# Second GIN pass of a graph network kernel: the second weight product for four chunks at a time

## The chip, the cores and the metric

The kernel runs on one core of one Trainium2 chip. The metric is the device time of one execution in microseconds. Nine plain executions of the kernel before took 5144.92 to 5174.38 us, with a median of 5162.2 us. Besides these there is one profiled execution, and every row quoted from the profile comes from it.

The engines are called as the profile calls them: PE is TensorE's matrix product (PEld its weight load), DVE is VectorE, ACT is ScalarE, POOL is GpSimd, SP is SyncE, which here only issues transfers. A name with q behind it (SPq) is the engine's sequencer.

## The reference

A graph has 6250 nodes with 256 features and 100,000 edges, sorted by destination. Two layers follow one another, each as `x = x + layer(relu(layernorm(x)))`. The first is an attention layer with batch norms. The second, which the change touches, is three graph convolutions (GIN):

```
def _gin_conv(h, src, dst, w, b, eps, n_nodes):
    agg = jax.ops.segment_sum(h[src], dst, num_segments=n_nodes)
    return ((1.0 + eps) * h + agg) @ w + b
h = relu(_gin_conv(x, src, dst, w1, b1, eps1, n))    # 256 -> 512
h = relu(_gin_conv(h, src, dst, w2, b2, eps2, n))    # 512 -> 512
return   _gin_conv(h, src, dst, w3, b3, eps3, n)     # 512 -> 256
```

For each node the features of all its neighbours are added up, its own features are added, and the sum goes through a weight matrix.

## The kernel before

The edges are cut into 53 chunks (`NCK`), each of 15 tiles (`CK`) of 128 edges, so that one chunk covers the edges of at most 128 destination nodes. For one tile, POOL issues an indirect DMA that gathers the 128 source rows from a table in DRAM into a row buffer `g` (`gather`, line 538). DVE makes, once a chunk, the matrix `hot` (line 555) that has a one where an edge belongs to a node. A product of `hot` with the gathered rows, accumulated over the 15 tiles in `sum`, gives the neighbours' sum for the chunk's nodes (`neighbours`, the products at line 1121; in f32 each shows as two product instructions and two weight loads).

The second layer is done in three passes over the chunks. The pass of this study (pools `s3`) is the second: its table `g1_d` has rows of 512 f32 numbers, 2 KB, so a tile's gather brings 256 KB. For each chunk, in the order of the program:

- SP loads the chunk's own rows (`own_rows`, line 1134, five buffers) and the rows of the residual (`x1`, line 1260, six buffers).
- `neighbours` runs the 15 gathers and products, with 24 row buffers `g`.
- DVE adds the own rows to the neighbours' sum (line 1263) into `own`.
- A step `flip` transposes `own` on TensorE (line 1145, four tiles of 128 columns), and ACT copies the result into the chunk's quarter or half of `tt` (line 1146).

The pass also applies the second weights, and at once the third ones, which stand before the third sum (the sum of products is the product of the sum). That is done by `layer23` for two chunks together. It makes steps: four `two(f)`, each with one tile of 128 outputs of the second product for all the nodes of both chunks (`h_ps`, line 1224, four accumulated products of 256 columns, then a relu by ACT into `g2`, line 1227); and one `three(q)` a chunk, with the third product (`y_ps`, line 1234, one buffer). After that product ACT copies `y` (line 1238), `apart` splits it into three bf16 parts (lines 1102 to 1105, ACT and DVE in turn), SP stores the parts as rows of `y3_d` (line 1244), and DVE adds the bias `g_b3` to `x1` (line 1245), then `y` times (1 + eps) (line 1246), and SP stores the result in `base_d` (line 1247). `keep_rows` (line 1209) loads finished rows of `y3_d` back into `tab`, for the last pass.

The steps are not run where they are made. They are put on the list `work`, and `neighbours` takes one from it after the products of the tiles named in `between`, ten of a chunk's 15:

```
between = (2, 4, 5, 6, 7, 8, 10, 11, 12, 13)
...
            if j in between and work:
                work.pop(0)()
```

So a chunk's `flip` runs after the third tile of the next chunk. With pairs, the even chunk (the first of a pair) carries seven steps: the flip of the chunk before, four `two` and two `three`, at tiles 2, 4, 5, 6, 7, 8 and 10. The odd chunk carries one flip. What is left at the end runs after the last chunk.

The order of instructions on an engine follows the program, except that the planner which builds the program puts an instruction earlier when it takes its inputs to be there. In the trace of before, the bias addition of line 1245 is one of these: it needs only `x1` and the bias, and stands ahead of the row addition (line 1263) of a chunk. `tc.keep_in_program_order` puts an instruction behind everything that the program has already given its engine.

Gathers are issued in order by POOL. Each needs a free row buffer, which is one whose product has been done. The queue of SP holds the loads and the stores of the pass in one order.

Of the kernel before, what the change touches and what calls it, by code (L numbers as in the profile page):

```python
# [33 lines left out]
FT = mybir.dt.float32  # L34
# [3 lines left out]
OP = mybir.AluOpType  # L38
# [5 lines left out]
P = 128  # L44
NN = 6250
NE = 100000
D = 256
# [6 lines left out]
NCK = 53  # L54
# [50 lines left out]
def gnn_kernel(ctx: ExitStack, tc: tile.TileContext, a: dict, out: bass.AP):  # L105
# [391 lines left out]
    with branch.Else():  # L497
        chunked(tc, a, out, t)
# [3 lines left out]
def chunked(ctx, tc, a, out, t):  # L502

    nc = tc.nc
# [3 lines left out]
    vs_d, x1_d, g0_d, g1_d, y3_d, base_d = t.vs_d, t.x1_d, t.g0_d, t.g1_d, t.y3_d, t.base_d  # L508
    sizes = [P] * (NCK - 1) + [LASTW]

    def first_nodes():

        got = {}

        def of(c, engine):
            if c in (0, NCK - 1):
                return 0 if c == 0 else NN - LASTW
            if c % 8 == 0 or c == 1:
                c0, c1 = c // 8 * 8, min(c // 8 * 8 + 8, NCK)
                if (engine, c) not in got:  # L520
                    _, regs = nc.values_load_multi_w_load_instructions(
                        t.nodes[0:1, c0:c1],
                        engines=[engine],
                        min_val=0,
                        max_val=NN - P,
                        skip_runtime_bounds_check_because="chunks whose rows go past the end take the general path",
                    )
                    got[engine, c] = True
                    got[engine] = regs
            return got[engine][c % 8]  # L530

        return of

    def ds(node, c):
        return bass.ds(node, sizes[c])

    def gather(to, table, c, j):
        nc.gpsimd.indirect_dma_start(  # L538
            out=to,
            out_offset=None,  # L540
            in_=table,
            in_offset=bass.IndirectOffsetOnAxis(ap=src_c[:, c, j : j + 1], axis=0),
        )
# [8 lines left out]
    def one_hot(pool, rule, c, dtype=FT, **more):  # L552

        hot = pool.tile([P, CK, P], dtype, name="hot", **more)
        nc.vector.tensor_tensor(  # L555
            hot,
            rule[:, None, :P].to_broadcast([P, CK, P]),
            loc_c[:, c, :][:, :, None].to_broadcast([P, CK, P]),
            op=OP.is_equal,
        )  # L560
        return hot
# [24 lines left out]
    with (  # L586
# [70 lines left out]
        def apart(s, q):  # L657
            nc.scalar.activation(s.hot_t[:, edges_of(q)], s.loc_r[:, edges_of(q)], AF.Square, bias=minus_p)
# [316 lines left out]
    with tc.tile_pool(name="s1b", bufs=2) as sp, tc.tile_pool(name="s1b_ps", bufs=4, space=PSUM) as pp:  # L975
        w_2 = weight(sp, "w_2", [a["L0_gnn_W2"]])
        for n, (c0, w) in enumerate(parts):
# [4 lines left out]
            for f in range(4):  # L982
                ps = pp.tile([P, 512], FT, name="ps")
# [9 lines left out]
            for f in range(2):  # L993
                ps = pp.tile([P, 512], FT, name="ps2")
# [55 lines left out]
    g_b3 = row(wp, "g_b3", a["L1_gnn_b3"], D)  # L1050
    rule = ruler(ctx.enter_context(tc.tile_pool(name="l1_rule", bufs=1, space=PSUM)))[0]
    hots = []
# [40 lines left out]
    def three(ps, weights, rows, start, stop):  # L1093

        rows = rows.rearrange("p k d -> p (k d)")
        parts = [(ps, rows[:, : 2 * D]), (ps[:, D:], rows[:, 2 * D :])]
        for k in (0, 1) if start else (1, 0):
            nc.tensor.matmul(parts[k][0], weights, parts[k][1], start=start and k == 0, stop=stop and k == 0)  # L1098
# [8 lines left out]
    def neighbours(pool, psum, table, c, n, bufs, hots, work, dense=None, dtype=FT):  # L1107


        if dense and c in dense.cs:  # L1110
            return dense.sums.pop(c)
        if c == 0:
            hots.append(one_hot(pool, rule, 0, dtype))
        hot = hots.pop()
        ps = psum.tile([P, n if dtype == FT else 2 * D], FT, name="sum")
        following = c + 2 if dense and c + 1 in dense.cs else c + 1
        for j in range(CK):
            g = pool.tile([P, n], dtype, name="g", bufs=bufs)
            gather(g, table, c, j)
            if dtype == FT:  # L1120
                nc.tensor.matmul(ps, hot[:, j, :], g, start=j == 0, stop=j == CK - 1)  # L1121
            else:
                three(ps, hot[:, j, :], g.rearrange("p (k d) -> p k d", k=3), j == 0, j == CK - 1)
            if j == 9 and following < NCK:
                hots.append(one_hot(pool, rule, following, dtype))
            if j in between and work:
                work.pop(0)()
            if dense:
                dense.step()
        return ps  # L1130

    def own_rows(pool, table, c, n, node):
        t = pool.tile([P, n], FT, name="own", bufs=5)
        nc.sync.dma_start(t[: sizes[c]], table[ds(node, c), :])
        return t
# [15 lines left out]
    with tc.tile_pool(name="s2", bufs=2) as sp, tc.tile_pool(name="s2_ps", bufs=2, space=PSUM) as pp:  # L1151
# [19 lines left out]
        work = [partial(part_rows, b0) for b0 in range(0, NFB, 5)]  # L1171
# [15 lines left out]
        for c in range(NCK):  # L1187
            R = slice(0, sizes[c])
            node = first(c, EN.SP)
            own = own_rows(sp, g0_d, c, D, node)  # L1190
            ps = neighbours(sp, pp, g0_d, c, D, 30, hots, work, dense)
# [3 lines left out]
            tt = sp.tile([P, 2, P], FT, name="tt")  # L1195
# [9 lines left out]
    def keep_rows(done):  # L1205

        while left and (left[0] + 1) * FB <= done:
            b = left.pop(0)
            nc.sync.dma_start(tab[:FB, b].rearrange("p k d -> p (k d)"), y3_d[b * FB : (b + 1) * FB, :])

    with tc.tile_pool(name="s3", bufs=2) as sp, tc.tile_pool(name="s3_ps", bufs=2, space=PSUM) as pp:
        first = first_nodes()
        work = []

        def layer23(cs, tt, nodes, x1s):

            n = sum(sizes[c] for c in cs)
            g2 = sp.tile([P, 4, 2 * P], FT, name="g2", bufs=1)
            tt_f = tt.rearrange("p f q n -> p f (q n)")

            def two(f):
                h_ps = pp.tile([P, 2 * P], FT, name="h_ps")
                for k in range(4):
                    nc.tensor.matmul(  # L1224
                        h_ps[:, :n], g_w2[:, k, f * P : (f + 1) * P], tt_f[:, k, :n], start=k == 0, stop=k == 3
                    )
                nc.scalar.activation(g2[:, f, :n], h_ps[:, :n], AF.Relu, bias=g_b2[:, f : f + 1])

            def three(q):
                c, node, x1 = cs[q], nodes[q], x1s[q]  # L1230
                R = slice(0, sizes[c])
                y_ps = pp.tile([P, D], FT, name="y_ps", bufs=1)
                for k in range(4):
                    nc.tensor.matmul(  # L1234
                        y_ps[R], g2[:, k, q * P : q * P + sizes[c]], g_w3[:, k, :], start=k == 0, stop=k == 3
                    )
                y = sp.tile([P, D], FT, name="y")
                nc.scalar.copy(y[R], y_ps[R])  # L1238
                y3 = sp.tile([P, 3, D], BF, name="y3")
                rest = sp.tile([P, D], FT, name="rest")  # L1240
                apart(y_ps[R], [y3[R, k, :] for k in range(3)], rest[R])
                if c:
                    keep_rows(DONE[c])
                nc.sync.dma_start(y3_d[ds(node, c), :], y3[R].rearrange("p k d -> p (k d)"))
                nc.vector.tensor_tensor(x1[R], x1[R], g_b3[R], op=OP.add)
                nc.vector.scalar_tensor_tensor(x1[R], y[R], eps1[R, 2:3], x1[R], op0=OP.mult, op1=OP.add)  # L1246
                nc.sync.dma_start(base_d[ds(node, c), :], x1[R])

            return [partial(two, f) for f in range(4)] + [partial(three, q) for q in range(len(cs))]

        for c0 in range(0, NCK, 2):
            cs = list(range(c0, min(c0 + 2, NCK)))
            tt = sp.tile([P, 4, 2, P], FT, name="tt")
            nodes, x1s = [], []
            for q, c in enumerate(cs):
                R = slice(0, sizes[c])
                nodes.append(first(c, EN.SP))
                own = own_rows(sp, g1_d, c, 2 * D, nodes[q])
                x1 = sp.tile([P, D], FT, name="x1", bufs=6)
                nc.sync.dma_start(x1[R], x1_d[ds(nodes[q], c), :])  # L1260
                x1s.append(x1)
                ps = neighbours(sp, pp, g1_d, c, 2 * D, 24, hots, work)
                nc.vector.scalar_tensor_tensor(own[R], own[R], eps1[R, 1:2], ps[R], op0=OP.mult, op1=OP.add)  # L1263
                work.append(flip_of(sp, pp, c, own, tt[:, :, q]))
            work += layer23(cs, tt, nodes, x1s)
        for f in work:
            f()

    with tc.tile_pool(name="s4", bufs=2) as sp, tc.tile_pool(name="s4_ps", bufs=2, space=PSUM) as pp:
# [3 lines left out]
        for c in range(NCK):  # L1273
            R = slice(0, sizes[c])
            node = first(c, EN.SP)
            o = own_rows(sp, base_d, c, D, node)
            ps = neighbours(sp, pp, y3_d, c, 3 * D, 30, hots, [], dense, BF)
# [779 lines left out]
```

## Time and profile before

| what | us |
|---|---|
| median of nine plain executions | 5162.2 |
| profiled execution, its own time | 5185.4 |
| its span, first to last instruction | 5183.6 |
| second GIN pass, first gather | 3078.9 |
| last gather of that pass issued | 4344.0 |
| first gather of the third pass | 4385.2 |
| PE busy in the span | 3496.0 |
| POOL busy in the span | 2819.9 |
| DVE busy in the span | 1644.2 |

In the profile, an instruction group or a timeline row names line, engine, operation, what is written and read, shape and count; times are the start in us and the length in us. In square brackets stands the time for which the engine stood idle before it, and what ended that: an instruction, a transfer (DMA), "issue" where the profile shows no wait, or "remote" where a semaphore changed at that time and the profile can't name who changed it. The ends of PE's products are modelled.

### The profile page before, as it was taken

The page shows a single profiled execution, that of the slowest core. Times are in us where ns is not written, and L with a number is a line of the kernel's source. Part 1 is how long each engine was busy: PE and PEld are TensorE (multiplying, and loading weights), DVE is VectorE, ACT ScalarE, POOL GpSimd, SP SyncE. Part 2 cuts the span into 40 slices and gives each one's busy share as a digit, 9 for nine tenths or more (in the row PEclk, how much of TensorE's full clock was granted, in tenths as well). Part 3 has the DMA queues.
Part 4 walks back from the last instruction along what each step waited for, and adds up shares of the span by engine and source line. Part 5 has one row for each costly group of instructions (what it writes and reads, how often), then busy time and mean ns, then how long its engine had stood idle before and what let it go on. Part 6 is the DMA issues. An engine that isn't in the chain of part 4 may idle for free.

```text
span 5183.6 us, 43522 instructions
## 1 busy us (share of the span) xinstructions
PE 3496.0 (67%) x14077; PEld 2104.0 (41%) x14077; DVE 1644.2 (32%) x3806; ACT 784.5 (15%) x1689; POOL 2819.9 (54%) x2947
## 2 busy tenths in 40 slices
PE   6725554555554008937888877888888887677777
PEld 3414433443433004625555544444444444233333
DVE  6536666666654004422111111111211211111111
ACT  2223333332332002211000000101101101000000
POOL 1355555554556760066666655565556554666665
PEclk8856777767776559968999998889989988788888
DMA  5466444443433002265555546676666665666665
GB/s 159 126 211 197 125 115 124 120 123 111 126 110 86 1 0 54 80 189 156 150 147 149 149 133 188 201 208 196 200 206 207 195 199 152 192 191 188 197 187 151
DMA packets 367412, 777.64 MB, mean 150 GB/s; under 512 B 83852, under 2 KB 197210, under 8 KB 366172
## 3 DMA queue, kind: packets, MB, share of 16 engines
q0 software_dynamic: 171120, 495.03, 33.6%
q1 hardware_dynamic: 172395, 261.51, 16.5%
q10 hardware_dynamic: 23658, 18.21, 1.2%
q8 instruction: 113, 1.85, 0.2%
q14 instruction: 126, 1.03, 0.1%
HBM read 703.07 MB, written 93.83 MB: 154 GB/s over the span
## 4 chain that ended last, share of the span: by engine, by line
PE 42%; another core or an unknown queue 20%; issue 16%; DVE 12%; DMA 6%; POOL 2%; ACT 2%; SPq 1%; ACTq 0%; DVEq 0%; POOLq 0%
PE dense L1098 10%; PE sum L1121 9%; PE sum L1098 4%; PE h_ps L1224 4%; PE acc L848 3%; DVE g L838 2%; PE g_ps L1179 2%; POOL g L538 2%; PE ps L985 2%; PE ps L996 2%; DVE junk L235 2%; PE y_ps L1234 1%; PE qk_ps L472 1%; DMA x<-x_d 1%
## 5 line engine op out<-in xcount | busy, mean ns | idle before, releaser
L538 POOL DMA_INDIRECT g<-g_d,src_t x1350 | 1287.9, 954 | 1137.0 <-PE sum L1121 319.8
L1121 PE MATMUL sum<-g,hot 128*128 128x512 f32 (+1 forms) x2700 | 1106.7, 531 | 59.8 <-DMA rows<-g_d 30.6
L538 POOL DMA_INDIRECT g<-vs_d,src_t x795 | 766.1, 964 | 682.4 <-issue 249.6
L848 PE MATMUL acc<-g,hot 128*128 128x264 f32 x1590 | 621.1, 546 | 514.1 <-DVE g L838 272.2
L1098 PE MATMUL dense<-tab,times 125*128 125x256 bf16 (+1 forms) x3300 | 792.0, 350 | 120.1 <-issue 116.9
L1121 PEld LDWEIGHTS sum<-g,hot 128*128 128x128 f32 x2700 | 532.7, 200 | 408.4 <-issue 352.2
L538 POOL DMA_INDIRECT g<-y_d,src_t x540 | 510.3, 945 | 307.9 <-PE dense L1098 113.8
L848 PEld LDWEIGHTS acc<-g,hot 128*128 128x128 f32 x1590 | 413.2, 278 | 610.0 <-DVE g L838 280.7
L1098 PEld LDWEIGHTS <-times 125*128 125x128 bf16 x3300 | 335.2, 103 | 457.0 <-issue 274.0
L1098 PE MATMUL sum<-g,hot 128*128 128x512 bf16 (+1 forms) x1080 | 303.6, 366 | 91.0 <-issue 68.9
L555 DVE TENSOR_TENSOR hot<-ruler,loc_t 128x1920 f32<-128x1920 f32 (+1 forms) x126 | 270.7, 2150 | 35.7 <-remote 13.1
L1224 PE MATMUL h_ps<-tt,g_w 128*128 128x256 f32 (+1 forms) x864 | 225.0, 408 | 61.8 <-issue 30.9
L1146 ACT COPY tt<-tp 128x256 f32<-128x256 f32 (+2 forms) x106 | 50.6, 478 | 1303.0 <-remote 673.3
L838 DVE TENSOR_TENSOR g<-g,at_ps 128x1024 f32<-128x1024 f32 x212 | 243.2, 1152 | 8.8 <-ACT at_ps L829 7.1
L1279 DVE TENSOR_TENSOR own<-own,sum 128x256 f32<-128x256 f32 (+1 forms) x72 | 30.0, 417 | 675.6 <-PE dense L1098 444.2
L253 POOL DMA_INDIRECT times<-val_t,at_t x210 | 205.1, 977 | 64.0 <-issue 64.0
L1224 PEld LDWEIGHTS h_ps<-tt,g_w 128*128 128x128 f32 x864 | 175.3, 209 | 156.7 <-issue 96.0
L1179 PE MATMUL g_ps<-g_w,tt 128*128 128x512 f32 (+1 forms) x212 | 133.7, 764 | 106.5 <-ACT tt L1146 59.0
L1098 PEld LDWEIGHTS <-hot 128*128 128x128 bf16 x1080 | 112.9, 106 | 210.7 <-issue 157.5
L1246 DVE SCALAR_TENSOR_TENSOR x<-y,eps,x 128x256 f32<-128x256 f32 (+1 forms) x53 | 25.7, 485 | 543.7 <-ACT y L1238 543.7
L1145 PE MATMUL tp<-ident,own 128*128 128x128 f32 (+1 forms) x318 | 65.2, 324 | 183.9 <-DVE own L1263 115.9
L677 PE MATMUL flip<-ident,s_e 128*120 128x128 f32 x53 | 18.6, 352 | 218.0 <-ACT s_e L672 187.2
(212 smaller groups left out, 3380.4 us busy)
## 6 DMA issues: line engine op xcount, KB each, us to landing
times<-times SPq DMA_DIRECT2D x165, 312.5 KB
loc_r<-loc_d SPq DMA_DIRECT2D x53, 480.0 KB
times<-zeros_d SPq DMA_DIRECT2D x14, 1562.5 KB
g<-g_d,src_t POOLq DMA_INDIRECT x1350
keys<-key_d SPq DMA_DIRECT2D x51, 384.0 KB
g_d<-g SPq DMA_DIRECT2D x52, 256.0 KB
own<-g_d SPq DMA_DIRECT2D x52, 256.0 KB
g<-vs_d,src_t POOLq DMA_INDIRECT x795
```

The costliest lines, as they stand in the source:

```text
L235: nc.vector.scalar_tensor_tensor(junk, keys[:, j * P : (j + 2) * P], key[:, q * 5 + j : q * 5 + j + 1], weigh, op0=OP.is_equal, op1=OP.mul ...
L253: return nc.gpsimd.indirect_dma_start(out=times_d[c], out_offset=bass.IndirectOffsetOnAxis(ap=at, axis=0), in_=val, in_offset=None)
L538: nc.gpsimd.indirect_dma_start(out=to, out_offset=None, in_=table, in_offset=bass.IndirectOffsetOnAxis(ap=src_c[:, c, j : j + 1], axis=0),)
L555: nc.vector.tensor_tensor(hot, rule[:, None, :P].to_broadcast([P, CK, P]), loc_c[:, c, :][:, :, None].to_broadcast([P, CK, P]), op=OP.is_e ...
L838: nc.vector.tensor_tensor(rows, rows, s.w_e[:, j0 // 8, j0 % 8 : j0 % 8 + n, :, None].to_broadcast([P, n, H, C]), op=OP.mult,)
L848: nc.tensor.matmul(s.acc, s.hot[:, j, :], s.g[:, j, :], start=j == 0, stop=j == CK - 1)
L985: nc.tensor.matmul(ps[:, :w], w_1[:, k, f * P : (f + 1) * P], h_t[:, k, c0 : c0 + w], start=k == 0, stop=k == 1,)
L996: nc.tensor.matmul(ps[:, :w], w_2[:, k, f * P : (f + 1) * P], hid[:, k, :w], start=k == 0, stop=k == 3)
L1098: nc.tensor.matmul(parts[k][0], weights, parts[k][1], start=start and k == 0, stop=stop and k == 0)
L1121: nc.tensor.matmul(ps, hot[:, j, :], g, start=j == 0, stop=j == CK - 1)
L1179: nc.tensor.matmul(g1_ps[R], tt[:, k, R], g_w1[:, k, :], start=k == 0, stop=k == 1)
L1224: nc.tensor.matmul(h_ps[:, :n], g_w2[:, k, f * P : (f + 1) * P], tt_f[:, k, :n], start=k == 0, stop=k == 3)
```

## The change

Three edits, all in the second GIN pass. `layer23` is given four chunks instead of two, so `h_ps`, `g2` and `tt` are twice as wide and the products at line 1224 have 512 columns; 53 chunks make 13 groups of four and one last chunk alone. To hold that, the row buffers go from 24 to 15, and the `x1` buffers from six to nine. And the bias addition is kept in its place in the program, behind the splitting of the product `y`.

```
         def layer23(cs, tt, nodes, x1s):
 
             n = sum(sizes[c] for c in cs)
-            g2 = sp.tile([P, 4, 2 * P], FT, name="g2", bufs=1)
+            g2 = sp.tile([P, 4, 4 * P], FT, name="g2", bufs=1)
             tt_f = tt.rearrange("p f q n -> p f (q n)")
 
             def two(f):
-                h_ps = pp.tile([P, 2 * P], FT, name="h_ps")
+                h_ps = pp.tile([P, 4 * P], FT, name="h_ps")
...
                 nc.sync.dma_start(y3_d[ds(node, c), :], y3[R].rearrange("p k d -> p (k d)"))
-                nc.vector.tensor_tensor(x1[R], x1[R], g_b3[R], op=OP.add)
+
+                tc.keep_in_program_order(nc.vector.tensor_tensor(x1[R], x1[R], g_b3[R], op=OP.add))
                 nc.vector.scalar_tensor_tensor(x1[R], y[R], eps1[R, 2:3], x1[R], op0=OP.mult, op1=OP.add)
...
-        for c0 in range(0, NCK, 2):
-            cs = list(range(c0, min(c0 + 2, NCK)))
-            tt = sp.tile([P, 4, 2, P], FT, name="tt")
+        for c0 in range(0, NCK, 4):
+            cs = list(range(c0, min(c0 + 4, NCK)))
+            tt = sp.tile([P, 4, 4, P], FT, name="tt")
...
-                x1 = sp.tile([P, D], FT, name="x1", bufs=6)
+                x1 = sp.tile([P, D], FT, name="x1", bufs=9)
...
-                ps = neighbours(sp, pp, g1_d, c, 2 * D, 24, hots, work)
+                ps = neighbours(sp, pp, g1_d, c, 2 * D, 15, hots, work)
```

With groups of four, the first chunk of a group carries nine steps: the flip of the chunk before, four `two` and four `three`, at tiles 2, 4, 5, 6, 7, 8, 10, 11 and 12. The other three chunks carry one flip each.

## The prediction

> **What bounds the kernel now.** The page first: 5183.6 us of span, 5185.4 us for the profiled execution. The nine plain times have a median of 5162.2 us, so the execution that I read is 0.45% above it, and the sum below is made against 5185.4 and then moved down by 23.
>
> ```profile
> span 5183.6 us, 43522 instructions
> PE 3496.0 (67%) x14077; PEld 2104.0 (41%) x14077; DVE 1644.2 (32%) x3806; ACT 784.5 (15%) x1689; POOL 2819.9 (54%) x2947
> PE   6725554555554008937888877888888887677777
> ```
>
> The change touches the second GIN pass alone, which runs from the first gather of `g1_d` at 3078.9 us to about 4385 us, a quarter of the span. Inside it I read the starts of the row addition at L1263, one a chunk. From chunk 4 (3227.65) to chunk 50 (4335.05) they are 1107.4 us apart, 48.15 us for two chunks. The two are unlike: 20.4 us on average from an even chunk's addition to the odd one's, where TensorE runs only gather products (L1121) and a transposition, and 27.7 us from odd to even, where the weight products of the pair before (L1224, L1234) lie between the gather products. Busy time by stretch, for one odd chunk, the even one after it, and the odd chunk 51, in which the last gathers end:
>
> ```profile
> 3707.95:3729.62 21.67, 15.85 (x40) 6.85 (x38) 3.67 (x5) 0.58 (x1) 15.10 (x16) 0.94 0.85 260
> 3729.62:3755.22 25.60, 23.20 (x77) 15.12 (x78) 5.30 (x9) 4.58 (x11) 13.22 (x14) 0.92 0.55 159
> 4335.05:4348.37 13.32, 13.32 (x35) 6.09 (x34) 2.82 (x3) 0.58 (x1) 7.57 (x8) 1.00 0.80 247
> ```
>
> The columns are length, then PE, PEld, DVE, ACT, POOL, clock, DMA share, GB/s. In the even chunk TensorE is nearly full. In the odd chunk it has 15.9 us of records in 21.7. Chunk 51 does an odd chunk's work in 13.3 us. The timeline shows why the others take 8 us more:
>
> ```profile
> 3710.76 13.04 PE L1121 MATMUL sum<-g,hot 128*128 128x512 f32 x30
> 3724.92 0.94 POOL L538 DMA_INDIRECT g<-g_d,src_t  x1 [0.89 <-PE sum L1121]
> 3727.03 0.94 POOL L538 DMA_INDIRECT g<-g_d,src_t  x1 [1.17 <-remote]
> 3729.62 0.75 DVE L1263 SCALAR_TENSOR_TENSOR own<-own,eps,sum 128x512 f32<-128x512 f32 x1 [3.49 <-remote]
> 3730.51 1.08 PE L1145 MATMUL tp<-ident,own 128*128 128x128 f32 x4 [6.71 <-issue]
> ...
> 4337.86 13.04 PE L1121 MATMUL sum<-g,hot 128*128 128x512 f32 x30
> 4348.37 0.75 DVE L1263 SCALAR_TENSOR_TENSOR own<-own,eps,sum 128x512 f32<-128x512 f32 x1 [10.50 <-PE sum L1121]
> ```
>
> Of the 30 products from 3710.76, 24 end the odd chunk (at about 3721.1) and six open the next, and then TensorE must transpose the odd chunk's `own`. L1263 needs the chunk's last product, but starts at 3729.6, 8.5 us after it; TensorE stands 6.7 us. What L1263 waits for, shown as remote, is the semaphore that counts TensorE's work, and POOL waits on it too. In chunk 51 the same 24 products end at 4348.2 and L1263 starts at once: POOL issued its last gather at 4344.0. So TensorE's completions become visible late while gathers are issued without pause (every 1.25 us, from about 3705.6), not otherwise. In even chunks, where POOL stands in front of full buffers, the delay is 0.6 us. Gathered rows are not what is missing: gather 390, issued at 3694.41, is used at 3721.06. I call the delay the late count; its cause is not in the trace.
>
> **The change, part by part.**
>
> *Wider product.* Eight h products of 256 columns take 1.73 us (3741.24 to the next gather product at 3742.97); 30 of 512 columns take 12.88, so eight take 3.43. Four chunks need 64 x 0.216 = 13.8 us of h products now and 32 x 0.429 = 13.7 us after. Nothing is gained: each weight load (0.19 us) already lies beside a product. The Trainium skill, page "TensorE: Matmul & The Clock Gate", section "Back-to-back issue gap", gives a sustained spacing of 81 ns at 128 columns and 131 ns at 512, less than in proportion. By that law 256 columns cost some 98 ns (an estimate), and the halved count would save a third of the 13.8 us, 60 us over 13 groups; the rows contradict it for this f32 product, and I go by the rows.
>
> *Where the dense work goes.* Now one chunk in two carries it; after, one in four, as nine steps (flip, four `two`, four `three`) in the ten slots. TensorE's work for four chunks, at full clock, is 51.5 (gather products) + 13.8 + 6.9 (y) + 1.7 (transpositions) = 73.9 us; now they take 2 x 48.15 = 96.3. Each odd chunk so loses 11.2 us: 7.1 in itself (20.4 against 13.3) and 4.0 in the chunk after (27.7 against 23.7; late copies of the transposed rows, slow clock after standing). After the change, for a group:
> - the dense chunk: 12.9 + 13.7 + 6.9 + 0.4 = 33.9; 4.0 of loss as now; and `y_ps` has one buffer, freed 1.43 us after the product (3700.87 to 3702.30), while after the change only one gather's products (0.86) lie between the second and third and the third and fourth `three`: 2 x 0.57 = 1.1. Sum 39.0.
> - the first gather-only chunk, as an odd chunk: 20.4.
> - the second and third, which no row shows: each follows a chunk that has itself stood. Lower end 15 x 1.25 = 18.75, POOL's unbroken pace with no late count to speak of. Upper end 28.5, the addition-to-addition time of the first two chunks of this pass (3111.11 to 3139.58), both gather-only. I take the odd chunk, the nearest row, 20.4, plus a slow start: after standing, four gather products took 3.06 us (3731.39) against 1.71, so 1.35 more: 21.8.
>
> Together 39.0 + 20.4 + 43.6 = 103.0 against 96.3: +6.7 us for each of 13 groups, +87 us. The ends: 96.9 gives +8 us, 116.4 gives +261.
>
> That slow start is the clock gate: the clock falls after the gap. The same page, Part 1, states half clock after about 3.4 us idle, and another 3.4 us of activity to leave it, 1.7 us lost each time instead of 1.35 (estimate); by it the two chunks cost 0.7 more a group, +9 us in all.
>
> *15 row buffers instead of 24.* A gather's rows are used under 5 us after its issue when TensorE waits for them (first issue 3078.92, first product 3083.78), and now rows lie landed for 20 us and more. 15 buffers are a whole chunk ahead. POOL's need is 60 x 1.25 = 75 us a group, less than 96. Taken at nothing; if the late count vanished, this would be the next bound. Lower end: POOL standing earlier shortens the late count (in the 18.75 above). Upper end: in the startup POOL ran 42 gathers before it stood, so fewer buffers bound nothing worse than 28.5.
>
> *Bias addition pinned.* Now L1245 runs ahead on DVE and waits for the `x1` load (11.39 us at 3725.7), in front of L1263. Over the pass DVE waits 331 us there, but L1263 then still waits for TensorE's count in 50 of 53 chunks, and the waits of TensorE put down to L1245 are 6.7 us, one. Gain: 7 us at least by that row, at most the three chunks times 11.4 = 34; I take 7. After the pin, L1245 (0.42) follows L1105 and precedes L1246, so the split of `y` (L1103, L1105) no longer stands behind L1246 and the base store goes out 1 us later; hidden by SP, which waits for the `tab` load anyway.
>
> *SP's queue.* The `y3` store, its `tab` load and the next `y3` store wait for each other: 3703.22, 3706.57, 3712.79, 3717.51, some 9.6 us a chunk. Four in a row hold the queue for 40 us; behind them are `own` and `x1` loads. `own` has five buffers, so a load comes four chunks ahead (some 80 us): hidden. `x1` with nine buffers reuses one that was stored a group earlier: hidden. At the end of the pass gathers have stopped, and a chunk's chain takes 5.8 us (4367.31 to 4373.10): four from the dense part of chunk 52 end near the last products; +2 us.
>
> *ACT.* L1227 on 512 columns costs as L1146's 0.58 us instead of 0.47, beside 3.4 us of product: nothing.
>
> Sum: +87 - 7 + 2 = +82; 5267 against the profiled execution, 5244 against the median. I say 5240.
>
> **The rivals.**
> - *POOL stands sooner and the late count shrinks (same or faster).* For it: with chunk 51, and the 0.6 us behind even chunks, the delay needs unbroken gathers, and 15 buffers end a run of gathers 9 earlier. Against: now, too, POOL starts an odd chunk at its buffer limit. Decides below: it ends faster once the two later gather-only chunks fall under 18.5 each; with the first one at 18.75 too, and 1.35 of clock, 39.0 + 3 x 18.75 = 95.3, -13 us, 5149; with no loss at all POOL's 75 us, -21 x 13 = -277, 4885. I expect some -60 in this case.
> - *Startup regime (much slower).* Gather-only chunks keep TensorE waiting and cold; 28.5 us twice a group: +261, 5420. For it: the two first chunks. Against: POOL had 24 free buffers then and no bound.
> - *The bias wait was the real stop.* If L1245 caused the stands, the pin would remove 7 us from each of 26 odd chunks, -180 us, and the group would win. Against: L1263 waited on TensorE 3.5 us longer than on DVE in the chunk shown, and chunk 0's addition came at 3111.1, its products having ended at 3101.4, with DVE idle since 3092.4.
> - *Nothing moves:* lower end of the third term, +8 us.
>
> **How the numbers follow.** Main case 0.55 (5190 to 5300), startup-like 0.13, near nothing 0.08, sooner-standing POOL 0.19, bias wait 0.05. A measurement tells some 0.2%, 10 us, from no change. Slower 0.69, same 0.08, faster 0.23. The range leaves out about one in ten on each side: below 5110 most of the strong gains, above 5350 the full startup regime.
>
> **What would show it.** L1263's starts in groups of one long (39) and three short gaps (20 to 22); TensorE standing 5 to 7 us before three of four transpositions, released as remote; 448 h products of twice the length and unchanged busy time; no L1245 wait for `x1`; gathers waiting for TensorE. Wrong if short gaps are below 18.5, if TensorE waits for gathers (buffers too few), or if SP's loads come late.

## The result, and the profile after

The changed kernel takes 5214.12 us (median of 17 executions, 5172.98 to 5233.29), the kernel before 5167.15 (median of 54): ratio 1.0084, 95% interval 1.0068 to 1.0101. So it is slower, by 47 us by the medians where 78 were forecast, and inside the range. The profiled execution took 5214.28 us, with these lines on its page:

```profile
span 5212.5 us, 42688 instructions
PE 3483.7 (67%) x13661; PEld 1985.1 (38%) x13661; DVE 1641.8 (31%) x3806; ACT 770.8 (15%) x1637; POOL 2816.5 (54%) x2947
PE   6634545555553129768888877788788787677777
```

TensorE has 12 us less to do than before (3496.0), and the span is 29 us longer. The pass as a whole, from its first gather to its last row addition, by stretch; first the kernel before, then the changed one (columns: stretch, length, then busy us and instructions of PE, PEld, DVE, ACT, POOL, then clock, DMA share, GB/s):

```profile
3078.90:4372.00 1293.10, 1069.70 (x3046) 596.20 (x3046) 234.28 (x314) 134.11 (x312) 752.65 (x795) 0.90 0.67 198
```

```profile
3053.20:4394.90 1341.70, 1064.36 (x2626) 483.30 (x2627) 229.69 (x309) 119.81 (x257) 751.99 (x795) 0.90 0.64 190
```

The pass is 48.6 us longer. TensorE's records fill 5 us less of it, so it stands 277 us instead of 223. That is the whole change: what comes before the pass ended 25.7 us sooner in this execution and what follows took 6 us longer, which is why the two spans differ by only 29.

The starts of the row addition (now line 1264) come in groups of four, as forecast, but with other lengths. From chunk 4 to 51 the means are 48.3 us for the dense chunk, then 15.3, 14.5 and 21.3; together 99.3 a group against 96.0 before. One group by stretch, from one row addition to the next (this one has a longer third and a shorter dense gap than most; the medians are 19.5 and 50.8); the columns are as above:

```profile
3596.02:3610.47 14.45, 14.45 (x41) 7.09 (x40) 4.93 (x8) 1.63 (x4) 10.38 (x11) 1.00 0.82 249
3610.47:3625.38 14.91, 14.91 (x39) 6.73 (x38) 2.82 (x3) 0.58 (x1) 8.61 (x10) 1.00 0.82 261
3625.38:3655.11 29.73, 17.95 (x37) 5.07 (x35) 2.81 (x3) 0.59 (x1) 22.56 (x24) 0.88 0.76 229
3655.11:3694.74 39.63, 35.01 (x88) 17.94 (x89) 7.25 (x13) 6.49 (x14) 15.11 (x16) 0.83 0.45 128
```

The first two gather-only chunks leave TensorE no gap at all. Rows picked from the timeline of the same group, in order of time:

```profile
3599.97 13.04 PE L1121 MATMUL sum<-g,hot 128*128 128x512 f32 x30
3613.28 13.04 PE L1121 MATMUL sum<-g,hot 128*128 128x512 f32 x30
3624.00 0.94 POOL L538 DMA_INDIRECT g<-g_d,src_t  x1 [3.33 <-PE sum L1121]
3625.38 0.75 DVE L1264 SCALAR_TENSOR_TENSOR own<-own,eps,sum 128x512 f32<-128x512 f32 x1 [12.09 <-PE sum L1121]
3627.94 3.48 PE L1121 MATMUL sum<-g,hot 128*128 128x512 f32 x6 [1.05 <-DMA g<-g_d,src_t]
3632.10 1.12 PE L1121 MATMUL sum<-g,hot 128*128 128x512 f32 x2 [0.68 <-DMA g<-g_d,src_t]
...
3645.29 1.13 PE L1121 MATMUL sum<-g,hot 128*128 128x512 f32 x2 [0.18 <-DMA g<-g_d,src_t]
3655.11 0.75 DVE L1264 SCALAR_TENSOR_TENSOR own<-own,eps,sum 128x512 f32<-128x512 f32 x1 [26.92 <-remote]
3656.00 1.08 PE L1145 MATMUL tp<-ident,own 128*128 128x128 f32 x4 [9.58 <-issue]
3660.96 0.94 POOL L538 DMA_INDIRECT g<-g_d,src_t  x1 [3.51 <-PE sum L1121]
3663.59 0.58 ACT L1146 COPY tt<-tp 128x512 f32<-128x512 f32 x1 [34.74 <-remote]
3664.23 5.82 PE L1224 MATMUL h_ps<-tt,g_w 128*128 128x512 f32 x8 [3.73 <-issue]
```

In the third gather-only chunk TensorE has caught up with POOL: it waits for gathers (DMA rows). POOL issues from 3624.0 to 3656.5 without a pause, and now the late count comes (that a signal of TensorE becomes visible some us after its product): the chunk's last products ended near 3646, the row addition starts at 3655.1, TensorE stands 9.6 us in front of the transpositions; and the copy of the transposed rows starts at 3663.6, 6.5 us after them, with the h products behind it. Of the waits between 3227 and 4290 us (total, times, longest):

```profile
POOL g L538 <- PE sum L1121: 249.5, 131, 5.5
PEld h_ps L1224 <- ACT tt L1146: 133.8, 8, 18.9
PE h_ps L1224 <- ACT tt L1146: 125.7, 8, 18.1
PEld sum L1121 <- DMA g<-g_d,src_t: 124.0, 149, 2.3
DVE own L1264 <- remote: 83.7, 4, 26.9
PE tp L1145 <- issue: 34.7, 6, 11.0
PE h_ps L1224 <- issue: 23.9, 3, 16.4
```

Eight times, in some eleven groups, the h products wait some 16 us for the copy into `tt`. In the kernel before, the same rows of the same stretch are:

```profile
PE tp L1145 <- DVE own L1263: 101.8, 17, 6.8
PE h_ps L1224 <- issue: 28.7, 14, 4.3
PE tp L1145 <- issue: 22.5, 5, 6.8
PE h_ps L1224 <- ACT tt L1146: 14.5, 3, 8.2
```

So TensorE stands less in front of the transpositions than before (35 us instead of 124, by all rows of this kind) and more in front of the h products (150 instead of 46). In front of gather products it stands 32 us, where before no such row is listed.

### The profile page after: what moved, and what is told of

Same layout as the page of the kernel before. It is cut to its first block, busy times and chain, and to the rows that moved or that the text cites. A ratio compares the mean times of both kernels' runs of the same rounds, so it can differ in the third digit from the quotient of the medians.

```text
span 5212.5 us, 42688 instructions
## 1 busy us (share of the span) xinstructions
PE 3483.7 (67%) x13661; PEld 1985.1 (38%) x13661; DVE 1641.8 (31%) x3806; ACT 770.8 (15%) x1637; POOL 2816.5 (54%) x2947
## 4 chain that ended last, share of the span: by engine, by line
PE 42%; another core or an unknown queue 22%; issue 13%; DVE 11%; DMA 5%; POOL 4%; ACT 1%; DVEq 0%; SPq 0%; ACTq 0%; POOLq 0%
PE sum L1121 11%; PE dense L1098 11%; PE sum L1098 4%; POOL g L538 4%; PE h_ps L1224 4%; PE acc L848 3%; DVE g L838 2%; PE g_ps L1179 2%; PE ps L985 2%; PE y_ps L1234 2%; PE ps L996 2%; DVE junk L235 1%; DMA times<-all_val,all_at 1%; DVE hot L644 1%
## 5 line engine op out<-in xcount | busy, mean ns | idle before, releaser
L1121 PEld LDWEIGHTS sum<-g,hot 128*128 128x128 f32 x2700 | 510.3, 197 | 555.2 <-issue 356.3
L1224 PE MATMUL h_ps<-tt,g_w 128*128 128x512 f32 (+1 forms) x448 | 219.0, 638 | 168.3 <-ACT tt L1146 144.4
L1264 DVE SCALAR_TENSOR_TENSOR own<-own,eps,sum 128x512 f32<-128x512 f32 (+1 forms) x53 | 39.5, 746 | 546.8 <-PE sum L1121 313.0
L1224 PEld LDWEIGHTS h_ps<-tt,g_w 128*128 128x128 f32 x448 | 92.0, 214 | 292.4 <-ACT tt L1146 155.1
L1103 DVE TENSOR_TENSOR rest<-y_ps,y 128x256 f32<-128x256 f32 (+1 forms) x53 | 22.5, 424 | 545.1 <-ACT y L1102 537.2
```

The costliest lines, as they stand in the source:

```text
L1224: nc.tensor.matmul(h_ps[:, :n], g_w2[:, k, f * P : (f + 1) * P], tt_f[:, k, :n], start=k == 0, stop=k == 3)
```

## The experiments

The runs of this section fell on four chips, and the main finding lies there, so it stands first. On three of them (5, 9 and 12) the kernel before takes 3976 us, on one (15) it takes 5158, as it did where the two profiles above were taken. I call the first kind "prompt" and the second "late". Ratios are always to the kernel before on the same chip.

### The changed kernel again (late chip)

> The changed kernel itself, once more. The four runs so far were made where the kernel before takes 3976 us instead of 5167, and where TensorE's count is never late (copies of transposed rows start 0.09 us after the last transposition, instead of 3 to 4.5). There the pin gave -24 us with pairs, and four chunks with 15 buffers and no pin +53. If pin and grouping add up: +53 - 24, some 4005 us, ratio 1.006 to 1.009. If the pin is worth nothing with nine x1 buffers: ratio 1.012. If the chip is one with the late count: 5214 and 1.007 to 1.010 as before.

5219.17 us, ratio 1.0118 (1.0082 to 1.0155). Row additions 49.9, 14.6, 14.7, 20.3; pass 1343.5 us. The result stands on another set of runs.

### The pin alone (prompt chip)

```
-                nc.vector.tensor_tensor(x1[R], x1[R], g_b3[R], op=OP.add)
+                tc.keep_in_program_order(nc.vector.tensor_tensor(x1[R], x1[R], g_b3[R], op=OP.add))
```

> The kernel before with the pinned bias addition alone. Late count (my prediction): DVE's waits in front of the bias addition for the x1 load go, but the row addition still waits for TensorE's count in the odd chunks, 6 to 9 us behind the last product; 7 us faster at the row that I took, at most 34: ratio 0.993 to 1.000. Bias wait as the real stop: odd chunks fall from 20.4 to about 13.5 us, 150 to 180 us faster: ratio 0.965 to 0.971. Pin as a burden (split of y no longer behind the addition, base store later): 0 to 10 us slower.

3952.99 us, ratio 0.9939 (0.9919 to 0.9958): 23 us faster. Two chunks of this kernel by stretch:

```profile
2732.64:2745.95 13.31, 13.31 (x35) 6.10 (x34) 2.82 (x2) 0.59 (x1) 10.19 (x11) 1.00 0.89 274
2745.95:2770.11 24.16, 24.08 (x83) 15.05 (x82) 6.22 (x11) 4.58 (x11) 18.37 (x20) 1.00 0.81 250
```

This is my odd chunk without any late count. In all of the 53 chunks the row addition starts within 0.1 us of the last product's end, although POOL issues up to 360 gathers in a row at a pitch under 1.45 us. So unbroken gathers do not make the count late on their own; the late chip is needed as well. A pair takes 37.7 us here, POOL's 30 x 1.25 = 37.5.

### 15 buffers in pairs, without the pin (prompt chip)

```
-                ps = neighbours(sp, pp, g1_d, c, 2 * D, 24, hots, work)
+                ps = neighbours(sp, pp, g1_d, c, 2 * D, 15, hots, work)
```

> The kernel before (pairs) with 15 row buffers instead of 24, nothing else. Late count with buffers at nothing (my prediction): an odd chunk begins with 15 landed rows, uses 15 in 13 us while POOL issues 10 more, so none is missing: ratio 0.997 to 1.003. Shortage of rows as what costs the change its time: some of the 43 us appear here already: ratio 1.004 to 1.01. POOL standing sooner shortens the late count: odd gaps fall from 20.4 towards 18.75, up to 40 us faster: ratio 0.992.

3973.27 us, ratio 0.9988 (0.9974 to 1.0001): nothing that can be told from no change. Its odd chunks are longer than those with the pin; by stretch, and the wait that does it (chunks of 2400 to 3220 us):

```profile
2744.01:2760.07 16.06, 15.85 (x40) 6.85 (x38) 3.58 (x4) 0.59 (x1) 12.24 (x13) 1.00 0.90 282
```

```profile
DVE x L1245 <- DMA x<-x_d: 263.9, 42, 13.4
```

DVE stands in front of the bias addition until `x1` has landed, and the row addition is queued behind it: 16.2 us an odd chunk against 13.3 with the pin. The even chunk gives back part of that (22.7 us against 24.4), so a group of four chunks takes 77.8 us instead of 75.4. On this prompt chip the third rival, the bias wait, is a real stop, of some 1.2 us a pair.

### Four chunks without the pin (prompt chip)

```
-                tc.keep_in_program_order(nc.vector.tensor_tensor(x1[R], x1[R], g_b3[R], op=OP.add))
+                nc.vector.tensor_tensor(x1[R], x1[R], g_b3[R], op=OP.add)
```

> The changed kernel without the pin. By my prediction: 7 us slower than the changed kernel, at most 34: ratio to the kernel before 1.009 to 1.015, and waits for the x1 load come back in front of the bias addition. If x1 loads come four chunks ahead through nine buffers, nothing waits for them and the pin is worth nothing: 1.007 to 1.009. If the bias wait was the real stop: 50 us or more slower.

4029.34 us, ratio 1.0129 (1.0107 to 1.0152). This lies in the range that I expected from the late count, but there is none on this chip, so the agreement is chance. Row additions 33.0, 20.5, 13.6, 13.8, a group of 80.9. The dense chunk takes what TensorE's work alone makes of it (33.9 in my working). The loss sits in the first gather-only chunk, and the wait names it:

```profile
DVE x L1246 <- DMA x<-x_d: 322.4, 42, 16.6
```

Nine `x1` buffers do not bring the load ahead. In the group around 2700 us SP issues it at 2702.09, behind `y3` stores, `tab` and base transfers of the `three` steps (from 2681.74 on), the bias addition starts at 2708.05, and the row addition behind it 5.2 us after the chunk's last product.

### Four chunks with 19 buffers (two prompt chips)

```
-                ps = neighbours(sp, pp, g1_d, c, 2 * D, 15, hots, work)
+                ps = neighbours(sp, pp, g1_d, c, 2 * D, 19, hots, work)
```

> The changed kernel with 19 row buffers instead of 15. If the loss is a shortage of rows at the end of the three gather-only chunks (POOL stands some 24 us in the dense chunk in front of 15 full buffers, then TensorE catches up with it in the third gather-only chunk): four more rows lie ready, 4 x 1.25 = 5 us a group, 13 groups, 65 us less than the change: some 5150, ratio to the kernel before 0.995 to 0.999. If it is the late count, which only waits for its place: POOL's unbroken run is as long and the delay is found once a group as it is now: 5200 to 5215, ratio 1.006 to 1.009, with the third gap shorter and the dense one longer.

> The changed kernel with 19 row buffers, a second time, because the first was made where the late count is absent (there ratio 0.9977). With the late count (kernel before at some 5160 us): if the changed kernel's loss is a shortage of rows in the third gather-only chunk, four more rows save 4 x 1.25 = 5 us a group, 13 groups: some 5155, ratio 0.997 to 1.002. If the late count only comes once a group, wherever POOL catches up: the third gap falls by some 5 us and the dense chunk's grows by as much: 5195 to 5220, ratio 1.007 to 1.012. Without the late count: 0.997 to 0.999 again.

3968.35 and 3969.9 us, ratios 0.9977 (0.9965 to 0.9990) and 0.9978 (0.9963 to 0.9994). Row additions 34.0, 14.5, 13.3, 13.7: a group of 75.4, POOL's 75. Grouping by four gains nothing over pairs there: with the pin both take 75.4 us for four chunks, and the pairs are 15 us shorter in all. The second run fell on another prompt chip. So whether four more buffers would mend the change on the late chip was not measured; nor was the changed kernel itself, with 15 buffers, on a prompt one.

### Pairs, 15 buffers and the pin (late chip)

The second and the first of the diffs above, both on the kernel before: the change without the grouping.

> The kernel before (pairs) with the pin and 15 row buffers: the changed kernel without the grouping. No late count: pairs with the pin run at POOL's pace (37.7 us a pair against 30 x 1.25 = 37.5) with 24 buffers; 15 without the pin cost nothing; so 3953 to 3960, ratio 0.993 to 0.996, and what the changed kernel is above that is the grouping. If 15 buffers are short for a dense chunk of 24 us even in pairs: ratio 0.998 to 1.002. With the late count: -7 to -34 us by my prediction, -150 or more if the bias wait was the real stop.

5149.75 us, ratio 0.9981 (0.9962 to 1.0000); its pass takes 1293.1 us, as before to the tenth, and odd chunks 20.5 and 20.7 us. The waits over the pass:

```profile
DVE own L1263 <- remote: 473.5, 25, 29.8
ACT tt L1146 <- PE sum L1121: 447.6, 22, 49.2
```

The row addition, no longer behind the bias addition, waits as long for TensorE's count: in odd chunks it starts 7.3 us behind the chunk's last product on average, against 6.8 in the kernel before. So on the late chip the bias wait lies inside the late count, and the pin gains nothing that can be told from no change. What the changed kernel is above this one, 5219.17 - 5149.75 = 69 us by the medians of the same chip, is the grouping, at 15 row buffers and with the `x1` buffers that it needs.

### The dense steps spread over all chunks (late chip)

```
-    def neighbours(pool, psum, table, c, n, bufs, hots, work, dense=None, dtype=FT):
+    def neighbours(pool, psum, table, c, n, bufs, hots, work, dense=None, dtype=FT, at=between):
...
-            if j in between and work:
+            if j in at and work:
...
-                ps = neighbours(sp, pp, g1_d, c, 2 * D, 24, hots, work)
+                ps = neighbours(sp, pp, g1_d, c, 2 * D, 24, hots, work, at=(5, 9, 11, 13))
```

> The kernel before (pairs) with the dense steps of the second pass spread over all chunks, in the slots at 5, 9, 11 and 13 (four steps a chunk), instead of ten slots in every other chunk. No late count: the pass is at POOL's pace of 1.25 us a gather but for a few us a pair that stands in front of the bias addition cost; odd gaps 18 to 19, even 19 to 20, 0 to 25 us faster: ratio 0.994 to 1.000. With the late count as a stand of TensorE in front of transpositions: they come later in the chunk, the stands shrink from 6 or 7 us to 1 or 2 in each odd chunk, 100 to 180 us faster: ratio 0.965 to 0.98. With the late count tied to unbroken gathers: it follows into every chunk, no gain or some loss: 0.995 to 1.01.

5032.9 us, ratio 0.9762 (0.9731 to 0.9794): 125 us faster than the kernel before and 186 faster than the changed one. Three chunks by stretch:

```profile
3686.40:3706.09 19.69, 18.86 (x55) 10.88 (x56) 3.52 (x6) 1.39 (x4) 12.62 (x14) 0.91 0.81 248
3706.09:3729.35 23.26, 20.02 (x62) 11.03 (x60) 5.22 (x8) 3.51 (x10) 15.67 (x17) 0.98 0.72 206
3729.35:3749.04 19.69, 18.80 (x53) 10.94 (x54) 3.57 (x6) 1.44 (x4) 12.67 (x14) 0.85 0.80 250
```

The count is late in nearly every chunk now (row additions 2 to 10 us behind the last product, even and odd), as the third expectation had it. But TensorE has only 0.8 to 3.2 us without a record in these chunks, because the transposition comes at the sixth tile instead of the third, and dense work lies in both chunks. Which of the two does more was not parted. So the late count costs time where little work stands between a chunk's last product and the first instruction that needs its sum. Grouping by four moves that the other way: three chunks in a row without cover, and then all of the dense work behind one late copy.

### Spread and pinned (prompt chip)

The diffs of the spreading and of the pin together.

> Pairs, the dense steps spread over all chunks (slots 5, 9, 11, 13), and the bias addition pinned; the kernel before otherwise. With the late count (kernel before at some 5160 us): the spreading alone gave 0.976; the pin alone some 8 us; if they add up, ratio 0.970 to 0.977. If the waits that the pin removes were covered by the late count in pairs and stand free in the spread form (DVE waits for x1 in front of the row addition there): 20 to 60 us more than the spreading alone, ratio 0.964 to 0.972. Without the late count (kernel before at some 3976 us): pins and spreading both lead to POOL's pace, ratio 0.992 to 0.996.

3956.38 us, ratio 0.9944 (0.9924 to 0.9963); row additions 19.3, 18.5, 19.1, 18.5, a group of 75.4. No better than the pin alone, which takes as long for four chunks; POOL needs 75.0 us for them and TensorE 73.9 in my working. The spreading alone was not run on a prompt chip, nor this kernel on the late one.

### Half the gathers (late chip)

```
-            g = pool.tile([P, n], dtype, name="g", bufs=bufs)
-            gather(g, table, c, j)
+            if n == 2 * D and dtype == FT and j % 2:
+                pass
+            else:
+                g = pool.tile([P, n], dtype, name="g", bufs=bufs)
+                gather(g, table, c, j)
```

> The kernel before with half of the gathers of the second pass: each row buffer serves two products, so the neighbours' sum is another; the number of products is the same. POOL's need falls from 37.5 to some 19 us a pair. No late count and POOL's pace as the bound: TensorE's 36.9 us a pair bounds next, so only 5 to 25 us faster, since the two lie that close. With the late count tied to gathers issued without pause: it vanishes, a pair falls from 48 to some 38 us, 200 to 270 us faster. With the late count tied to something else: odd chunks still stand 6 to 8 us, at most 50 us faster.

Each row buffer serves two products here, so the sums are others, but the number of products is the same. 4856.71 us in one execution against 5157.81: 301 us less. Two chunks by stretch, an odd and the even one before it:

```profile
3690.19:3713.07 22.88, 21.44 (x78) 14.37 (x78) 5.64 (x10) 4.58 (x11) 5.83 (x7) 1.00 0.37 102
3713.07:3727.65 14.58, 14.58 (x38) 6.65 (x37) 3.59 (x5) 0.59 (x1) 7.37 (x9) 1.00 0.81 239
```

From the third chunk on no row addition comes more than 3.1 us behind its last product, most within 1.3; the odd chunk shown has no stand, and four chunks take 74.4 us, where my working gave TensorE's work alone 73.9. On the late chip the delay is tied to the gathers.

### Half the bytes, and half the gathers as plain loads (prompt chips)

These two were to part the issuing of gathers from the bytes that they move.

```
-            gather(g, table, c, j)
+            if n == 2 * D and dtype == FT:
+                gather(g[:, :D], g0_d, c, j)
...
```

(the product then reads the half row twice), and

```
-            gather(g, table, c, j)
+            if n == 2 * D and dtype == FT and j % 2:
+                nc.sync.dma_start(g, table[c * 112 : c * 112 + P, :])
+            else:
+                gather(g, table, c, j)
```

> The kernel before, with gathers of half the bytes in the second pass (1 KB a row instead of 2 KB, and the product reads it twice, so half of the columns hold other sums); as many gathers and products. If the late count comes from POOL's issuing of gathers: odd chunks still take 20 to 22 us, time within 50 us of the kernel before. If it comes from the bytes that the gathers move: the stands shrink to half or vanish, as they did with half the gathers (-301 us): 120 to 300 us faster. Without the late count at all (kernel before at some 3976 us): within 25 us.

> The kernel before, with every second gather of the second pass replaced by a plain load of 128 consecutive rows from SP's queue: the same bytes into the same buffers, half the gathers from POOL; so half of the rows that are summed are others. With the late count (kernel before at some 5160 us): if it comes from POOL's issuing of gathers, it vanishes as with half the gathers, 200 to 300 us faster, unless SP's loads come late behind its waits for y3 (then TensorE waits for rows and not for its count). If it comes from the bytes moved, odd chunks stand as before: within 60 us. Without the late count: within 30 us.

3946.99 us against 3975.62, and 3945.07 against 3977.37, one execution each; both fell on prompt chips, where there is no late count to take away. Four chunks take 75.2 us in both. They only show how close POOL and TensorE lie: with POOL's issuing halved in the second the chunks take no less, so the 75 us of the prompt chips is not shown to be POOL's pace alone; TensorE's 73.9 us is next to it. What in a gather makes the count late stays open.

## Why the prediction was right, and where it was not

**The direction held, and so did its root.** I had put TensorE's stands down to a count that becomes visible late while POOL issues gathers without pause. The change adds to them (223 to 277 us of standing in the pass), and in pairs half the gathers leave 20 us of them (1003.0 us of pass, 982.7 busy). The grouping itself costs 69 us on the late chip, the other two edits together nothing that is surely told from no change (0.9981, to 1.0000).

**The place did not.** I forecast stands of 5 to 7 us in front of three of four transpositions. In the stretch of the two waits tables these stands fell from 124 to 35 us; those in front of the h products rose from 46 to 150, and waits for gathers came on top (32 us). Two of my three signs of being wrong came true: short gaps under 18.5 us, and TensorE waiting for gathers. (A reading was wrong as well: in even chunks of the kernel before the row addition follows the last product by 0.04 us, not 0.6.)

**The size was off by 31 us** (78 forecast, 47 measured), and the step that failed is the split over the chunks. That the sum still came near is partly luck: the dense chunk was put 9.3 us too low and the gather-only ones together 12.9 us too high.

| step | forecast | measured (mean) |
|---|---|---|
| dense chunk | 39.0 | 48.3 |
| first gather-only chunk, "as an odd chunk" | 20.4 | 15.3 |
| second | 21.8 | 14.5 |
| third | 21.8 | 21.3 |
| sum for a group | 103.0 | 99.3 |

A group costs 3.3 us more than before instead of 6.7, so 13 groups cost 43 us instead of 87; the ramps of the pass bring the measured sum to 48.6. I charged the late count to each gather-only chunk. It is paid mostly at the end of a group. With 15 buffers POOL stands in the dense chunk, and in the group shown its first pause afterwards (3619.7 to 3624.0) lets the count catch up. From chunk 4 to 51 the row additions of the first two gather-only chunks start only 0.9 and 1.4 us behind their last products on average, that of the third 4.3; why the first is on time, no run shows. That such chunks would be short was in the rival "POOL stands sooner", and its mark, short gaps under 18.5, came true for two of the three. But the delay is then paid in the third chunk and, what I had not priced, in the dense chunk: there the late copy into `tt` holds up all the h products of four chunks, 125.7 us in eight places. The clock adds to it: in the group shown the dense chunk has a granted clock of 0.83, and its first eight h products take 5.82 us, the next eight 3.60. I had carried over 4.0 us of loss for this from the pairs.

**15 buffers at nothing was wrong for the group.** I counted a chunk of lead and POOL's 75 us against 96. But three gather-only chunks use 45 gathers in 3 x 13.3 = 40 us, in which POOL issues 32; the difference of 13 has to lie ready, and beside the rows still in flight and in use 15 buffers leave nothing over. TensorE did wait for gathers, which I had named as a sign against me. The late count has a part in it too, because it also tells POOL that a buffer is free: the gather of 3624.00 goes into the buffer of a product that had ended at 3614.3, and in the second gather-only chunk POOL stands 3.2 us a group for buffers whose products were done. How much of the shortage comes from the number of buffers is argued from my count and not shown: on the late chip no other number was run with groups of four, and on the prompt chips 19 buffers leave the third chunk at 13.7 us. In pairs the step was right: one gather-only chunk, 0.9988 and 0.9981 with 15 buffers.

**The pin** was put at 7 us; pairs with pin and 15 buffers gave 8, with no change as an end of the interval. That the bias wait was not the real stop holds on the late chip only: on a prompt chip it delays the row additions of odd chunks, and the pin alone brings 23 us.

**The wider product** gained next to nothing, as the rows said: 448 products of 219.0 us against 864 of 225.0. The Trainium skill, page "TensorE: Matmul & The Clock Gate", section "Back-to-back issue gap", would have had 60 us saved (estimate); 6 us of busy time went.

**SP and y_ps:** with the pin no row addition waited for a load of `own` or `x1`; without it, four chunks in a row on SP's queue do make `x1` late (322.4 us of waits on the prompt chip), which my step on SP's queue had called hidden. The 1.1 us for `y_ps` did not come: the third products start 3.44 us apart (3683.62, 3687.07, 3690.51, 3693.95), so two tiles of gather products lie between any two of them, where the list of steps has one in two of the three places.

## What to carry to other kernels

Before you group work to make instructions wider, ask what the scattered work was covering: here bunching the dense steps put the weight products of four chunks behind one late copy, which cost more than fewer, longer products gave (6 us of busy time). When consumers outrun a producer for several chunks, count whether the buffers hold the whole shortfall and what is in flight, not one chunk. And a wait that the trace puts on a semaphore long after its instruction ended may belong to the chip that the profile came from: spread work so that no single count is urgent, which helped most there (0.976) and, with the pin, lost nothing where counts were prompt (0.9944 against 0.9939 for the pin alone, each against the kernel before on its chip).

## What the runs showed of the hardware

The kernel before took 3976 us on three chips and 5158 on a fourth. Its profile on a late chip and that of the pin alone on a prompt one show hardly a difference in POOL's pace (1.25 us a gather), in the shortest time from a gather's issue to the product with its rows (3.7 and 3.6 us) or in the time that the gathers' packets took (33.6% of 5183.6 us on 16 engines against 42.8% of 3954.8, 1742 and 1693 us). What these profiles show to differ is when signals become visible. Counted from the records of semaphore updates in the trace, in some stretches of 5 us (due are the signals of TensorE's instructions that ended in the stretch):

```
kernel, chip               from     gathers  TensorE's signals   all signals
                           us       issued   due / recorded      recorded
before, late               3705     4        6 / 4               65
                           3710     4        8 / 3               24
                           3715     4        6 / 1               13
                           3720     4        5 / 2               11
changed, late              3615     4        6 / 1               10
                           3620     1        6 / 13              22
                           3645     4        2 / 0                8
half the gathers, late     3715     3        6 / 5               89
                           3725     3        7 / 7               76
pin alone, prompt          2725     4        6 / 6               77
                           2735     4        9 / 9              100
```

On the late chip the recorded signals of all engines and of the DMAs thin out after some 5 us of unbroken gathers, to about one of TensorE's in 5 us, and come in a burst when POOL pauses (13 in the stretch from 3620). In the records of the prompt chip they do not. Over the whole program 5213 of TensorE's 6255 signals are in the records of the kernel before on the late chip, 6244 with the pin alone on the prompt one; of the DMAs' 19831 against 63850. The instructions that wait start when a record says so (in the changed kernel a signal of TensorE is recorded at 3655.09 and the row addition starts at 3655.11), so the delay is not one of the recording alone. Only some 284 of the 1229 us between these two profiles lie in the second GIN pass; 829 us lie ahead of it and were not followed. Whether signals are merged or the record of some is lost, what the late chip lacks, and whether the bytes or the issuing of a gather fill the path, no run here tells.
